# A four-layer decoder: bfloat16 parts of queries and keys, their way through DRAM, and the order of score banks

## The chip, the cores and the metric

The kernel runs on one core of one Trainium2 chip. The time is device microseconds (us) of that core, from one launch to its end. TensorE multiplies (PE in the profile), VectorE (DVE) and ScalarE (ACT) read its results from the PSUM banks, GpSimd (POOL) works on SBUF alone, and SyncE (SP) does nothing but issue DMAs, in a fixed order.

## What is computed

Four decoder layers on x of shape (4, 256, 128), each with self attention, a second attention on a context of 512 rows (or of x on it), and a feed-forward part, with residual sums and a layer norm without weights ahead of each. The change touches the attentions with 16 heads of width 8, above all those of layers 0 and 3:

```python
x = x + _L0_attn_ref(_layernorm(x, axis=-1), ...)
x = x + _L0_xattn_ref(_layernorm(x, axis=-1), ctx_1024, mask_BxS2_bk0, ...)
x = x + _L0_ffn_ref(_layernorm(x, axis=-1), ...)
...
x = x + _L3_attn_ref(_layernorm(x, axis=-1), L3_attn_mask, ...)
x = x + _L3_xattn_ref(_layernorm(x, axis=-1), ctx_1024, ctx_1024, mask_1x1xSxS2_if1, ...)
x = x + _L3_ffn_ref(_layernorm(x, axis=-1), ...)
```

and each attention is of this form:

```python
attn = jnp.einsum('bhqd,bhkd->bhqk', q, k) * scale
attn = jnp.where(mask, attn, -inf)
attn = jax.nn.softmax(attn, axis=-1)
out = jnp.einsum('bhqk,bhkd->bhqd', attn, v)
```

Self attention has 256 keys, attention on the context 512. Layer 1's self attention clips its scores at ±10 and so needs no maximum.

## The kernel before

`woven` (line 428) runs the attentions of one layer. A *unit* is one attention of one of the four batch elements: in layers 0 and 3 units 0 to 3 are self attention and 4 to 7 attention on the context; in layer 1 there are only the four self units.

**Two passes over the scores.** `rows_of` makes scores with queries on the partitions, and VectorE takes each row's maximum from them (L568, or L572 with a mask added). `parts` (L606 to L610) cuts the maximum into three bfloat16 pieces in `mp`, and `parts_T` transposes these on TensorE (L618 or L631). `columns_of` makes the same scores again with keys on the partitions, less the maximum, and ScalarE takes the exponential (L675). `weighted` (L708) multiplies it with the values, `divided_by_sums`, `transposed_result` and `added` end the unit.

**Slots and beats.** Slot n is the time of unit n's columns. Beside them run the rows of unit n+1, all but the first two half groups, and the first two half groups (`LEAD`) of unit n+2. A *beat* is one half group of rows with one half group of columns: two banks of each, on four different quarters of 32 rows of TensorE's array, which work side by side. A slot has 8 beats where both units have 256 keys, 16 with 512. `front(n)` puts the `prelude` of unit n+2 (its norm on POOL, transposes, query and key products) into the first 0.4 of the slot (0.55 with 512 keys), so that its rows can begin in the slot's last two beats.

**Parts.** A float32 matmul is slow on TensorE. In layers 0 and 3 (`split=True`) all units but the first take their scores from bfloat16 matmuls instead. ScalarE writes queries and keys in float32; POOL cuts each into three bfloat16 parts (`in_parts`, L470 to L473). A feature of a head needs three partitions for the key parts (i = 0, 1, 2) and a fourth for the maximum; the query has three planes c, each repeated on the three partitions. So the parts have to move between partitions, and go through DRAM: one DMA writes the query parts (L494), nine read them (L497, one for each plane and i), one writes the key parts (L515), three read them (L517); the row mask of the context goes into the fourth partition (L521). What the fourth partitions hold otherwise comes from the constant `rest`, by four loads for each of three buffers at the start (L461). A score is then three matmuls, one for each query plane (`part`, L579 for rows and L681 for columns). For columns the third plane is `qmax`: `parts_T` adds the maximum's pieces to a copy of it (L624).

A unit without parts masks the queries to one head on POOL (`qm`, L503), has one float32 matmul for a score (L561 for rows, L658 for columns), and for columns two more with bfloat16 pieces of the maximum (`less`, L652).

**What sets the order.** Each function of a slot has a place between 0 and 1, and `run` calls them sorted by it; a layer under the program places instructions on their engines' queues and makes the waits. SP issues in its own fixed order. The four loads of layer 0's expert weights into `e0h` (L2283, 1 MB each) are one of these functions, in slot 0. The buffers of the parts lie in memory lent by tiles that aren't in use yet (`Lent`): `e0h` in layer 0, `cn` and `w2kv` in layer 3, the rest in the pool as `kk` and `q`. So a tile named `e0h` in an attention's line is a buffer of parts.

**Banks.** `ps("s1")` takes the next of seven PSUM banks in rotation; a bank is free again when its reader is done. In `beat` (L763) the steps are called one after the other, and each takes its two banks; the matmuls then go in rounds over the steps, and the reads in pairs: first bank of the rows, first of the columns, second of the rows, second of the columns.

Of the kernel before, what the change touches and what calls it, by code (L numbers as in the profile page):

```python
# [26 lines left out]
F32 = mybir.dt.float32  # L27
# [9 lines left out]
P = 128  # L37
# [64 lines left out]
def _layout(i):  # L102
# [19 lines left out]
    halves = np.concatenate([np.where(d < 3, 0xBF80, 0), 0 * d, np.where(d == 3, 0x3F80, 0)])  # L122
    a["rest"] = np.tile((halves * 0x10001).astype(np.uint32).view(np.int32), (1, 2 * SK))
# [76 lines left out]
def decoder(ctx: ExitStack, tc: tile.TileContext, dr, out):  # L200
# [227 lines left out]
    def woven(pool, units, n_keys, split=False, lent=None):  # L428
# [4 lines left out]
        for i in range(2):  # L433
            t = pool.tile([P, n_keys // P, H, 32], F32, tag=f"v{i}", name=f"v{i}", bufs=1)
            V.memset(t, 0.0)
            V.memset(t[:, :, :, HD : HD + 1], 1.0)
            vbuf.append(t)
            shape = [P, 2, 4, 4, 32] if split else [P, 2, 4, 32]
            t = pool.tile(shape, BF16, tag=f"mp{i}", name=f"mp{i}", bufs=1)
            V.memset(t, 0.0)  # L440
            mbuf.append(t)
        if split:
            mfirst = pool.tile([P, 2, 4, 32], BF16, tag="mp", name="mp", bufs=1)
            V.memset(mfirst, 0.0)

        kbuf, qbuf, kd, qd = [], [], [], []
        for i in range(3 if split else 0):
            def kept(what, n):
                t = lent.pop(4 * n)
                if t is None:  # L450
                    return pool.tile([P, 4, n], BF16, tag=f"{what}{i}", name=f"{what}{i}", bufs=1)
                return t.rearrange("p (g n) -> p g n", g=4)

            kbuf.append(kept("kk", n_keys))
            qbuf.append([kept(f"q{c}", S) for c in range(3)])
            kd.append(dram.tile([3, P, n_keys], BF16, tag=f"kp{i}", name="kp"))
            qd.append(dram.tile([3, P, S], BF16, tag=f"qp{i}", name="qp"))
            for c, t in enumerate(kbuf[-1:] + qbuf[-1]):
                n = 4 * t.shape[2] // 2
                m = 32 * (0, 1, 1, 2)[c]  # L460
                nc.sync.dma_start(  # L461
                    t.bitcast(I32).rearrange("p g n -> p (g n)")[3::4],
                    dr["rest"][m : m + 32, :n],
# [15 lines left out]
        def queries(u):  # L479
# [11 lines left out]
            if u.split:  # L491
                u.q3 = qbuf[u.n % 3]
                to = qd[u.n % 3]
                nc.sync.dma_start(to.rearrange("c f n -> f c n"), in_parts(q, "qp", S))  # L494
                for c in range(3):
                    for i in range(3):
                        nc.sync.dma_start(  # L497
                            u.q3[c][i::4], to[c].rearrange("(x g) n -> x g n", g=4)
                        )
                return  # L500
            u.qm = pool.tile([P, 4, S], F32, tag="qm", name="qm", bufs=1 if split else 3)
# [3 lines left out]
        def keys(u):  # L505
            acc = product(u.weights[1], u.key_source, "s1")
            u.kc = pool.tile([P, u.nk], F32, tag="kc", name="kc", bufs=2 if split else 3)
            if u.k_bias is None:
                A.copy(u.kc, acc)
            else:  # L510
                A.activation(u.kc, acc, AF.Identity, bias=u.k_bias)
            if u.split:
                u.kk = kbuf[u.n % 3]
                to = kd[u.n % 3][:, :, : u.nk]
                nc.sync.dma_start(to.rearrange("c f n -> f c n"), in_parts(u.kc, "kp", SK))  # L515
                for c in range(3):
                    nc.sync.dma_start(  # L517
                        u.kk[c::4, :, : u.nk], to[c].rearrange("(x g) n -> x g n", g=4)
                    )
                if u.row_mask is not None:  # L520
                    nc.sync.dma_start(  # L521
                        u.kk[15::32, :, : u.nk],
                        u.row_mask[0:4].unsqueeze(1).to_broadcast([4, 4, u.nk]),
                    )

# [18 lines left out]
        def rows_of(u, qt, g, half):  # L544
# [5 lines left out]
            rounds, reads = {}, []  # L550
            for j, r in row_tiles(half):
# [1828 lines left out]
```

## Time and profile before

| | |
|---|---|
| three runs | 1535.40, 1537.69, 1541.26 us |
| median | 1537.69 us |
| the profiled execution | 1537.51 us, its span 1535.40 us |
| mean granted TensorE clock | 0.901 of full |
| TensorE busy (matmuls) | 1283.8 us, 84% |
| VectorE, ScalarE, GpSimd busy | 826.5, 721.7, 325.8 us |
| moved by DMA | 89.85 MB, 59 GB/s on average |

The span has these stages, by the names of the tiles in the timeline: layer 0's attentions from about 10 to 280 us, its experts to 360, layer 1 with its experts to 630, layer 2 to 1190, and layer 3 from there to the end. In forty slices of 38.4 us, busy tenths of TensorE, VectorE and ScalarE, and the granted clock:

```profile
PE   3677889797886999889999999999597488898894
DVE  6367877385565345755444544442333555776743
ACT  0243555566552334257766756666121034345463
PEclk9688999897887999999999999999698579999996
```

A 9 is 90% or more of a slice. The first seven slices are layer 0's attentions, the last nine layer 3. TensorE's clock is granted in two steps, full and half, so a tenth below 9 in the fourth line means that part of the slice ran at half clock.

### The profile page before, as it was taken

The numbers are of one execution on the slowest core, as the hardware profiler recorded it, in microseconds if no ns is written. First come the engines' busy times: TensorE is split into PE (matmuls) and PEld (weight loads), VectorE is DVE, ScalarE is ACT, GpSimd is POOL, SyncE is SP. The second block draws the span as 40 slices with busy tenths as digits, with TensorE's granted clock in tenths as the row PEclk, the third lists the DMA queues.
The fourth block names the chain that finished last, engine by engine and source line by source line (L and its number), as shares of the span: only waits on it lengthen the run. The fifth ranks groups of instructions, "written<-read, shape, count | busy, mean of one in ns | idle before, by whom it ended". The sixth has DMA issues, their size and how long they took to land.

```text
span 1535.4 us, 29900 instructions
## 1 busy us (share of the span) xinstructions
PE 1283.8 (84%) x11340; PEld 708.6 (46%) x11340; DVE 826.5 (54%) x2697; ACT 721.7 (47%) x1461; POOL 325.8 (21%) x489
## 2 busy tenths in 40 slices
PE   3677889797886999889999999999597488898894
PEld 2244444344344565645555555455365234344442
DVE  6367877385565345755444544442333555776743
ACT  0243555566552334257766756666121034345463
POOL 6133220155022315100000000000231613322000
PEclk9688999897887999999999999999698579999996
DMA  4232110331051216050110000000312211211000
GB/s 149 75 116 73 53 47 5 148 122 36 1 216 38 75 35 214 28 179 15 56 42 19 28 5 4 1 8 5 126 39 67 66 32 42 72 44 43 5 5 7
DMA packets 57263, 89.85 MB, mean 59 GB/s; under 512 B 8853, under 2 KB 35711, under 8 KB 55455
## 3 DMA queue, kind: packets, MB, share of 16 engines
q1 hardware_dynamic: 52706, 71.59, 14.1%
q0 software_dynamic: 3264, 6.69, 2.0%
q10 hardware_dynamic: 1152, 9.67, 1.6%
q8 instruction: 91, 1.49, 0.4%
q14 instruction: 50, 0.41, 0.1%
HBM read 64.10 MB, written 23.75 MB: 57 GB/s over the span
## 4 chain that ended last, share of the span: by engine, by line
PE 62%; DVE 12%; POOL 7%; ACT 6%; issue 5%; DMA 5%; SPq 2%; ACTq 0%; POOLq 0%; DVEq 0%
PE o L708 6%; PE o L2041 6%; PE g L1300 6%; PE s L579 5%; PE s L2021 5%; PE f L1967 4%; PE s L681 3%; PE y L1324 3%; PE s L645 2%; PE f L1953 2%; POOL xn L318 2%; PE s L360 2%; DVE mx L568 2%; POOL back L1373 2%; PE t L1309 2%
## 5 line engine op out<-in xcount | busy, mean ns | idle before, releaser
L675 ACT ACTIVATE pr<-s 128x512 f32<-128x512 f32 x384 | 206.4, 597 | 272.5 <-PE s L681 196.7
L310 POOL TENSOR_SCALAR ve<-mv 128x2 f32<-128x2 f32 x44 | 11.7, 267 | 776.7 <-DVE mv L305 771.2
L568 DVE TENSOR_REDUCE mx<-s 128x1 f32<-128x512 f32 (+1 forms) x192 | 122.2, 684 | 78.3 <-PE s L681 38.8
L1978 ACT ACTIVATE ss<-ss,ntop 128x768 f32<-128x768 f32 x128 | 118.6, 928 | 88.5 <-DVE ntop L1976 88.2
L708 PE MATMUL o<-pr,v 128*32 128x256 f32 (+1 forms) x1792 | 149.1, 404 | 7.4 <-ACT os L714 6.2
L1972 DVE CUSTOM_DVE_ANT_0 ss<-f,n 128x512 f32<-128x512 f32 x128 | 83.6, 689 | 73.7 <-PE f L1967 73.7
L579 PE MATMUL s<-e0h 32*128 32x512 bf16 (+1 forms) x672 | 80.6, 370 | 41.7 <-DMA e0h<-kp 37.1
L2041 PE MATMUL o<-pr,v 128*64 128x256 f32 x768 | 107.1, 392 | 1.2 <-ACT pr L2028 1.2
L572 DVE CUSTOM_DVE_ANT_0 junk<-s,nmif 128x512 bf16<-128x512 f32 x128 | 82.9, 687 | 37.8 <-PE s L681 30.1
L2021 PE MATMUL s<-qT,kT 64*128 64x256 f32 x768 | 101.5, 379 | 0.0
L2028 ACT ACTIVATE pr<-s,n 128x512 f32<-128x512 f32 x128 | 80.3, 679 | 24.5 <-PE s L2021 24.3
L1967 PE MATMUL f<-kT,qT 64*128 64x512 f32 x256 | 79.7, 637 | 3.7 <-ACT kT L290 2.0
L1278 POOL DMA_INDIRECT xb<-sent,token x62 | 59.8, 964 | 105.4 <-PE t L1285 58.8
L2041 PEld LDWEIGHTS o<-pr,v 128*64 128x64 f32 x768 | 48.0, 136 | 56.6 <-issue 20.3
L708 PEld LDWEIGHTS o<-pr,v 128*32 128x32 f32 x1792 | 41.4, 111 | 67.2 <-issue 45.5
L1960 DVE CUSTOM_DVE_ANT_0 ss<-f,nought 128x256 f32<-128x256 f32 x128 | 46.7, 421 | 46.7 <-PE f L1953 46.2
L2021 PEld LDWEIGHTS s<-qT,kT 64*128 64x128 f32 x768 | 67.8, 189 | 5.8
L572 DVE CUSTOM_DVE_ANT_0 junk<-s,nmcau 128x256 bf16<-128x256 f32 x128 | 46.4, 421 | 37.8 <-PE s L658 16.9
L579 PEld LDWEIGHTS <-e0h 32*128 32x128 bf16 x672 | 28.0, 100 | 76.0 <-issue 72.5
L681 PE MATMUL s<-e0h 32*128 32x256 bf16 x704 | 58.6, 283 | 4.8 <-DVE mx L568 4.6
L328 PE MATMUL s<-consts,xn 128*128 128x128 f32 x64 | 19.5, 361 | 47.2 <-POOL xn L318 47.2
L318 POOL TENSOR_SCALAR xn<-x,mv,rs 128x128 f32<-128x128 f32 x72 | 57.6, 807 | 3.8
(489 smaller groups left out, 2730.4 us busy)
## 6 DMA issues: line engine op xcount, KB each, us to landing
kd<-ahead SPq DMA_DIRECT2D x20, 256.0 KB
vd<-ahead SPq DMA_DIRECT2D x20, 256.0 KB
kT<-kd SPq DMA_DIRECT2D x20, 256.0 KB
v<-vd SPq DMA_DIRECT2D x5, 1024.0 KB
e0h<-in_e0h SPq DMA_DIRECT2D x4, 1024.0 KB
e0h<-in_e0h SPq DMA_DIRECT2D x1, 4096.0 KB
e0d<-in_e0d SPq DMA_DIRECT2D x2, 2048.0 KB
e1h<-in_e1h ACTq DMA_DIRECT2D x1, 4096.0 KB
```

The source lines that it names most:

```text
L318: (on or V).tensor_scalar(d, s, mv[:, i, 0:1], rs[:, i : i + 1], ALU.subtract, ALU.mult)
L568: V.tensor_reduce(u.mx[:, qt, j, g : g + per], sc, AX.X, ALU.max)
L572: V.tensor_tensor_reduce(junk[:, : u.nk], sc[:, i, :], u.rows_mask(qt), 1.0, -3e38, ALU.add, ALU.max, accum_out=u.mx[:, qt, j, g + i : g + ...
L579: T.matmul(sc[:, i, :], lhsT=u.q3[c][r, g + i, qt * P : (qt + 1) * P], rhs=u.kk[r, g + i, : u.nk], start=n == 0, stop=n == 3 * per - 1,)
L675: A.activation(dst, sc, AF.Exp)
L681: T.matmul(sc[:, i, :], lhsT=u.kk[r, gp + i, kt * P : (kt + 1) * P], rhs=(u.q3[0], u.q3[1], u.qmax)[c][r, gp + i, :], start=u.cols_mask is ...
L708: T.matmul(u.po[gp][32 * j : 32 * j + 32, i, first:], lhsT=u.v[:, kt, 4 * j + gp + i, :], rhs=u.pr[gp, kt, j][:, i, first:], start=kt + i ...
L1300: T.matmul(p[r], lhsT=xbT[b][:, r], rhs=w(512 * i), start=biases is None, stop=True,)
L1967: T.matmul(sc[h], lhsT=qT[u, c][hrow[h], qt * P : (qt + 1) * P], rhs=kT[u, c][hrow[h], :SK], start=True, stop=True,)
L1978: A.activation(ss[qt][h], ss[qt][h], AF.Exp, bias=ntop[:, qt, h, c : c + 1], accum_out=total[:, qt, h, c : c + 1],)
L2021: T.matmul(sc[h][:, i, :], lhsT=kT[u, c][hrow[h], kt * P : (kt + 1) * P], rhs=qT[u, c][hrow[h], :], start=False, stop=i == 1,)
L2041: T.matmul(po[u, g][hrow[h], i, :], lhsT=v[u][:, kt, n * hd : (n + 1) * hd], rhs=pr[u, g, kt, h][:, i, :], start=kt + i == 0, stop=kt + i ...
```

## The change

- Only units from 2 on are split into parts; unit 1 of layers 0 and 3 is computed as unit 0 is.
- In DRAM the parts now lie as they will lie in SBUF: partition 4x + i, and in it for the queries head group, plane and query in a row. Queries take three writes (one for each i, the same data) and one read, keys three writes (one for each part) and one read. The fourth partitions' constants are written into DRAM once for all three buffers, and the row mask goes there too, ahead of the read.
- The maximum's pieces are added to the third plane in place; `qmax` is gone. `mp3` is one tile for all split units. The float32 keys of split units have one buffer (`kf`).
- In a slot, the norm of unit n+3 comes at 0.8, and the rest of a split unit's prelude ends at 0.35 (0.5 with 512 keys) instead of 0.4 (0.55).
- `rows_of` and `columns_of` return a function for each bank instead of all banks; `beat` calls them in turn, one of either step, so banks are taken in the order in which they are read, and the matmuls of a round alternate between rows and columns.

```diff
+    words = [(h * 0x10001).astype(np.uint32).view(np.int32) for h in (
+        np.where(d < 3, 0xBF80, 0), np.where(d == 3, 0x3F80, 0)
+    )]
+    a["restk"] = np.tile(words[0], (1, 2 * SK))
+    n = np.arange(4 * 3 * S // 2)[None, :] // (S // 2) % 3
+    a["restq"] = np.where(n == 2, words[1], 0).astype(np.int32)
...
-    def woven(pool, units, n_keys, split=False, lent=None):
+    def woven(pool, units, n_keys, split=None, lent=None):
...
-            for c, t in enumerate(kbuf[-1:] + qbuf[-1]):
-                n = 4 * t.shape[2] // 2
-                m = 32 * (0, 1, 1, 2)[c]
+        if split:
+            kd = dram.tile([3, 32, 4, 4 * n_keys], BF16, tag=f"kp{split}", name="kp")
+            qd = dram.tile([3, 32, 4, 12 * S], BF16, tag=f"qp{split}", name="qp")
+            for i in range(3):
+                kbuf.append(kept(f"kk{i}", 4 * n_keys).rearrange("p (g n) -> p g n", g=4))
+                qbuf.append(kept(f"qq{i}", 12 * S).rearrange("p (g c n) -> p g c n", g=4, c=3))
+            for t, r in ((kd, dr["restk"]), (qd, dr["restq"])):
                 nc.sync.dma_start(
-                    t.bitcast(I32).rearrange("p g n -> p (g n)")[3::4],
-                    dr["rest"][m : m + 32, :n],
+                    t.bitcast(I32)[:, :, 3], r.unsqueeze(0).to_broadcast([3, 32, r.shape[1]])
                 )
...
             if u.split:
                 u.q3 = qbuf[u.n % 3]
-                to = qd[u.n % 3]
-                nc.sync.dma_start(to.rearrange("c f n -> f c n"), in_parts(q, "qp", S))
-                for c in range(3):
-                    for i in range(3):
-                        nc.sync.dma_start(
-                            u.q3[c][i::4], to[c].rearrange("(x g) n -> x g n", g=4)
-                        )
+                to, t = qd[u.n % 3], in_parts(q, "qp", S).rearrange("p c n -> p (c n)")
+                for i in range(3):
+                    nc.sync.dma_start(to[:, i].rearrange("x (g n) -> x g n", g=4), t)
+                nc.sync.dma_start(
+                    u.q3.rearrange("p g c n -> p (g c n)"), to.rearrange("x i n -> (x i) n")
+                )
                 return
-            u.qm = pool.tile([P, 4, S], F32, tag="qm", name="qm", bufs=1 if split else 3)
+            u.qm = pool.tile([P, 4, S], F32, tag="qm", name="qm", bufs=2 if split else 3)
...
             if u.split:
                 u.kk = kbuf[u.n % 3]
-                to = kd[u.n % 3][:, :, : u.nk]
-                nc.sync.dma_start(to.rearrange("c f n -> f c n"), in_parts(u.kc, "kp", SK))
-                for c in range(3):
-                    nc.sync.dma_start(
-                        u.kk[c::4, :, : u.nk], to[c].rearrange("(x g) n -> x g n", g=4)
-                    )
+                to = kd[u.n % 3].rearrange("x i (g n) -> x i g n", g=4)[:, :, :, : u.nk]
+                t = in_parts(kc, "kp", SK)
+                for i in range(3):
+                    nc.sync.dma_start(to[:, i], t[:, i])
                 if u.row_mask is not None:
                     nc.sync.dma_start(
-                        u.kk[15::32, :, : u.nk],
+                        to[3::8, 3],
                         u.row_mask[0:4].unsqueeze(1).to_broadcast([4, 4, u.nk]),
                     )
+                nc.sync.dma_start(u.kk[:, :, : u.nk], to.rearrange("x i g n -> (x i) g n"))
...
-                u.qmax = pool.tile([P, 4, S], BF16, tag="qmax", name="qmax")
-                V.tensor_tensor(
-                    u.qmax, tp.rearrange("p (g n) -> p g n", g=4), u.q3[2], ALU.add
-                )
+                third = u.q3[:, :, 2, :]
+                V.tensor_tensor(third, tp.rearrange("p (g n) -> p g n", g=4), third, ALU.add)
                 return
...
-            made = [f(half) for f, half in steps]
+            pairs = zip(*[f(half) for f, half in steps])
+            made = [f() for pair in pairs for f in pair]
...
-            for pair in zip(*[m[2] for m in made]):
-                for f in pair:
-                    f()
+            for _, _, read in made:
+                read()
...
-                end = 0.95 - lead if not u.split else 0.4 if units[n].nk < SK else 0.55
-                out += spread(prelude(u), 0.0, end)
+                if u.split:
+                    end = 0.35 if units[n].nk < SK else 0.5
+                    out += spread(prelude(u)[1 if n else 0 :], 0.0, end)
+                else:
+                    out += spread(prelude(u), 0.0, 0.95 - lead)
+            if split and n + 3 < len(units):
+                out += [(0.8, prelude(units[n + 3])[0])]
...
-            u.n, u.split = n, split and n > 0
+            u.n, u.split = n, bool(split) and n > 1
...
-            first += spread(prelude(units[1]), 0.0, 0.3 if split else 0.8)
+            first += spread(prelude(units[1]), 0.0, 0.8)
```

## The prediction

> **What bounds the kernel now.** I read the page for the span and the engine shares, then the waits, then PE's timeline over the two stages that call `woven` with parts (layer 0, about 10 to 280 us, and layer 3, about 1190 us to the end), then SP's timeline for one unit, then windows around one stop.
>
> ```profile
> PE 1283.8 (84%) x11340; PEld 708.6 (46%) x11340; DVE 826.5 (54%) x2697; ACT 721.7 (47%) x1461; POOL 325.8 (21%) x489
> L579 PE MATMUL s<-e0h 32*128 32x512 bf16 (+1 forms) x672 | 80.6, 370 | 41.7 <-DMA e0h<-kp 37.1
> ```
>
> TensorE is the engine that carries the span, and the score rows (L579) are the one group that stands idle on a DMA. The tile view of kp gives PE's whole wait on it as 55.4 us in 10 stops. PE's timeline shows the stops:
>
> ```profile
> 45.16 1.25 PE L579 MATMUL s<-e0h 32*128 32x256 bf16 x19 [13.17 <-DMA e0h<-kp]
> 72.76 0.39 PE L579 MATMUL s<-e0h 32*128 32x256 bf16 x2 [5.88 <-DMA e0h<-kp]
> 101.25 0.39 PE L579 MATMUL s<-e0h 32*128 32x256 bf16 x2 [7.32 <-DMA e0h<-kp]
> 128.35 0.61 PE L579 MATMUL s<-e0h 32*128 32x512 bf16 x2 [6.84 <-DMA e0h<-kp]
> 192.04 0.61 PE L579 MATMUL s<-e0h 32*128 32x512 bf16 x2 [3.50 <-DMA e0h<-kp]
> 229.35 0.61 PE L579 MATMUL s<-e0h 32*128 32x512 bf16 x2 [4.62 <-DMA sent<-xn]
> 1256.19 0.40 PE L579 MATMUL s<-kk,q 32*128 32x256 bf16 x2 [5.42 <-DMA kk<-kp]
> 1286.14 0.39 PE L579 MATMUL s<-cn 32*128 32x256 bf16 x2 [7.00 <-DMA cn<-kp]
> 1315.03 0.61 PE L579 MATMUL s<-w2kv 32*128 32x512 bf16 x2 [5.38 <-DMA w2kv<-kp]
> ```
>
> Each is the first row matmul of a new unit; in brackets is how long PE stood before it. Their sum is 59.1 us, 41.3 in layer 0 and 17.8 in layer 3. (The one put down to `sent` has SP's three kp reads issued just ahead of it; I count it as theirs.) Why the parts are late is on SP:
>
> ```profile
> 114.20 0.36 SPq L494 DMA_DIRECT2D qp<-qp  x1
> 116.17 5.59 SPq L497 DMA_DIRECT2D e0h<-qp  x9
> 121.86 0.53 SPq L515 DMA_DIRECT2D kp<-kp  x1
> 124.50 1.72 SPq L517 DMA_DIRECT2D e0h<-kp  x3
> ```
>
> Query write, 1.97 us until its nine reads may issue, 5.59 us to issue them, then the key write behind them, though POOL had the key parts at 117.9; 2.64 us to land, three reads, and PE starts at 128.35: 14.15 us. A stop costs twice, as the granted clock (last but two column) shows around the one at 66.9 to 72.8:
>
> ```profile
> 70.00:72.00 2.00, 0.00 (x0) 0.00 (x0) 0.00 (x0) 0.00 (x0) 0.00 (x0) 0.92 0.27 79
> 72.00:74.00 2.00, 1.24 (x18) 0.94 (x20) 0.00 (x0) 0.00 (x0) 0.00 (x0) 0.50 0.37 72
> 76.00:78.00 2.00, 2.00 (x17) 0.84 (x19) 1.68 (x5) 0.27 (x1) 0.00 (x0) 0.50 1.04 430
> 78.00:80.00 2.00, 2.00 (x31) 0.90 (x24) 0.41 (x1) 0.56 (x2) 0.00 (x0) 0.87 0.98 414
> ```
>
> **What the skill says.** The Trainium skill, "TensorE: Matmul & The Clock Gate", "What's actually happening": after an idle window of about 3.4 us the array gets half its clock, and full clock again after a busy one. The trace agrees: 0.50 from the stop until about 78.5. "DMA: Bandwidth & Descriptors", "Anatomy of one DMA — SWDGE (gpsimd) path": a DMA costs about 2.0 us plus its bytes at 436 GB/s, most of the fixed part being the wait for the write's receipt. The page fits another issuing path, but here 192 KB of queries takes 1.97 us and the 384 KB key write 2.64, and the windows move 414 to 430 GB/s; I use 2.0 and 430. The page's "Rules for kernel authors" say to coalesce many small transfers into one large; the one read does that.
>
> **The change part by part.**
>
> *Units split.* Unit 1 of either layer stays in float32. The 13.17 us stop goes, but its rows still wait for VectorE: in the trace the last row reduction of unit 0 ends at 35.0; four banks of unit 1 at 0.64 us (L568) and the copy of mT follow, so slot 0 can start at about 38.7 instead of 49.4: 10.7 gained. In layer 3 unit 1 had no DMA stop. Price: the columns of unit 1. A beat's score matmuls take 0.84 us when both sides are parts (81.77 to 82.61) and 1.34 with float32 columns (62.50 to 63.84): 0.5 x 8 beats x 2 layers = 8. Mixed float32 rows and columns in slot 0 I put at 0.15 x 6 x 2 = 1.8 more, an estimate: the second row matmul stands ahead of the column's second correction in PE's order. Six transposes less per layer give back 1.6. On POOL, four masks of queries (3.63) replace eight part operations (4.2 to 4.3): nothing. In layer 3 they stand behind the norm of unit 2 and its gathers in POOL's order: I allow 2 us. Sum +10.
>
> *Writes and reads.* Per split unit the queries take three writes and one read in place of one and nine; the keys three and one in place of one and three. From POOL's finished queries (at 430 GB/s, issues 0.36 to 0.53 us as in the trace): three writes issue in 1.1 and land at 2.7; the read issues until 3.3 and moves 786 KB, landing at about 7.1. Key parts are ready at 3.7, each write waits for its own part, the last issues by 4.6 and lands at about 7; the read of 524 KB issues by 7.6 and lands at 7.6 + 1.2 + about 1.7 = 10.5. That is 3.6 less than 14.15. Bounds: 9 if nothing queues on the rings, 16 if the wider reads move at the 105 GB/s of the nine small ones (576 KB in 5.59 us). I take 10.5, since the 430 GB/s windows show large rows at full rate.
>
> *Begun sooner.* The norm moves to 0.8 of the slot before, and in PE's order both products come one beat sooner: about 2.0 us. With 3.6 this covers 5.6 us of each stop. But full clock at a slot's head also shortens the slot before the parts are needed. Counting beats from the key product to the first row of the unit: unit 3 of layer 0 has 4 x 1.25 + 3.6 of weighted sums + 2 = 10.6 us against a chain of 9 to 10; unit 4 has 8.0 against 0.7 + 3.6 + 2.6 + 0.5 + 3.2 = 10.6. Unit 2's reads now stand behind the first 1 MB load of `e0h` (2.4 us). Left over: unit 2 about 2, unit 3 about 1, unit 4 about 2.6; in layer 3 about 0, 0.5 and 2; the later cross units none (3.50 and 4.62 are under 5.6). So 8 us stay, and of 59.1 go 59.1 - 2.5 (VectorE, unit 1) - 8 = 48.6. The other three `e0h` loads (3 MB, 7.5 us) now precede unit 3's writes on their semaphores, but more than a slot's half lies between: nothing; if the cover went, up to 7 us.
>
> *Clock.* Behind the stops before, PE worked at half clock for 5.8, 4.65, 4.85, 6.0, 6.25 (layer 0) and 3.4, 4.3, 6.0 us (layer 3): 41.3. Half would be lost if PE alone set the pace; I take 0.4: 16.5. Slot 0 of layer 0 stood at half clock until about 61.6: five beats at 3.4 us (52.23 to 55.63) that take 2.56 warm (62.50 to 65.06): 4.3. Less 3 for the stops left over: 17.8. The head of layer 3 keeps its low clock (0.51 over 1180 to 1240), where VectorE waits for gathers.
>
> *Bank order, and the rest.* Banks are now allocated as they are read, so a reused bank frees in order. PE's waits on readers at L579 and L681 are about 25 us in all, few of them of this kind: -3 to +1, taken as 0. The third plane is added in place; were the first plane's matmuls to wait for it too, 0.5 us x 12 units: 0 to +6, taken as 0, since the list has under 3 us for the wait on `qmax`. `kf` has one buffer instead of two, but its next writer comes a slot later: nothing. One more `evacuate` swaps VectorE and ScalarE for the copies between the two layers; both have slack there (PE's digit is 9 in most of those slices of the page): -2 to +2.
>
> Sum: 48.6 + 17.8 - 10 = 56. The profiled execution took 1537.51 us with a span of 1535.40, 2.1 around it, and the median shown is 1537.69: 1537.5 - 56 = 1481.5, so **1482 us**. A check: layer 0 from 40 to 240 us has VectorE busy for 132.2 us. It loses about 44 of its 200 us; 132/156 is 85%, and the undisturbed stretch 140 to 180 already has 34.7 of 40 (87%). So this is near the next bound, and much more is not to be had there.
>
> **The rivals.**
>
> *Half of it stays.* PE reaches the row beats sooner than counted, so most split units still stop 2 to 4 us, long enough to halve the clock. For it: unit 4's count; against: 5.6 us per unit. Nine stops of 3 us and their clock: 27 + 9 left instead of 8 + 3, so gain 56 - 25 = 31: 1507.
>
> *All of it goes.* No stop is left, and the clock stays: 56 + 11 = 67, and bank order gives 3 to 8: about 1465. VectorE's 87% speaks against it.
>
> *Slower.* The threefold writes and the wide reads move at the small reads' 105 GB/s. Per unit 590 + 786 + 393 + 524 KB = 2.3 MB: 22 us and two receipts of 2: 26 against 14.15. Twelve units, less the 2 us begun sooner, late by 10 more each, 120, less the 25 that unit 1 gives: about 1620. It decides once the chain passes about 17 us: 2.9 more than 14.15, less 2.0, in 12 units is 11, as much as unit 1's gain after its price. Below some 180 GB/s it wins; the windows with 414 to 430 speak against.
>
> **How the numbers follow.** Forecast 0.62 (1465 to 1500), half of it 0.19, all of it 0.09, slower 0.06, no change 0.04 (the gains met by VectorE). The range 1458 to 1512 holds the first three but for their edges. This kernel's runs tell 0.5%, some 8 us, from no change: faster 0.90, same 0.04, slower 0.06.
>
> **What would show it.** PE's line at L579 with DMA waits under 15 us in all instead of 55; SP's chain from the first query write to the key read's landing near 10.5; no cold stretch in slot 0 of layer 0; beats of unit 1's columns near 1.3 us. It is wrong if stops of over 3 us stay before unit 3 or 4, if the single reads take over 6 us to land, or if VectorE is over 90% busy in layer 0.

## The result

The changed kernel takes 1518.4 us (median of four runs, 1512.65 to 1520.42) beside 1537.0 (1535.40 to 1541.26): ratio 0.9869, 95% interval 0.9835 to 0.9902, so 18.6 us faster where 56 were forecast. The profiled execution took 1517.87, its span 1516.0, with a mean granted clock of 0.912. From the page after (engine shares; then the group of row matmuls, with its idle time and releaser last):

```profile
PE 1292.0 (85%) x11200; PEld 709.5 (47%) x11200; DVE 821.6 (54%) x2696; ACT 722.7 (48%) x1462; POOL 324.1 (21%) x481
...
L582 PE MATMUL s<-e0h 32*128 32x512 bf16 (+1 forms) x576 | 73.0, 365 | 18.8 <-DMA e0h<-kp 18.3
```

and PE's timeline after, each line the first row matmul of a unit:

```profile
61.11 0.37 PE L582 MATMUL s<-e0h 32*128 32x256 bf16 x1 [5.08 <-DMA e0h<-kp]
92.57 0.37 PE L582 MATMUL s<-e0h 32*128 32x256 bf16 x1 [5.26 <-DMA e0h<-kp]
117.67 0.58 PE L582 MATMUL s<-e0h 32*128 32x512 bf16 x1 [5.48 <-DMA e0h<-kp]
179.97 0.48 PE L582 MATMUL s<-e0h 32*128 32x512 bf16 x1 [2.46 <-DMA e0h<-kp]
1241.58 0.33 PE L582 MATMUL s<-kk,qq 32*128 32x256 bf16 x1 [2.47 <-DMA kk<-kp]
1268.58 0.26 PE L582 MATMUL s<-cn,w2kv 32*128 32x256 bf16 x1 [2.25 <-DMA cn<-kp]
1293.72 0.58 PE L582 MATMUL s<-cn,qq 32*128 32x512 bf16 x1 [2.78 <-DMA cn<-kp]
```

These are units 2, 3, 4 and 6 of layer 0 and 2, 3, 4 of layer 3: 25.8 us of stops beside 59.1 before. The forecast left 8.

A stop is a difference of two times, both counted from the first query write on SP: the *chain*, until the parts have landed, less the *cover*, until PE has nothing else to do. Read off SP's and PE's timelines (us; layer 3's units with a dash ahead):

```
             unit:    2      3      4      6      7     -2     -3     -4
before      chain  14.03  14.66  14.15  14.67  15.29  13.89  14.22  14.71
            cover   8.15   7.34   7.31  11.17  10.67   8.47   7.22   9.33
after       chain  13.07  17.07  11.17  14.71     no   8.87  12.78  11.04
            cover   7.99  11.81   5.69  12.25   stop   6.40  10.53   8.26
```

Forecast were a chain of 10.5 and 2.0 more cover everywhere. Over the seven units that still stop the chain went from 14.3 to 12.7 and the cover from 8.4 to 9.0: 2.2 us off each stop, not 5.6. (Unit 7, whose stop went, is not in these means.) And the longest chain is longer than any before. SP's timeline after, for unit 3 of layer 0:

```profile
75.50 1.85 SPq L496 DMA_DIRECT2D qp<-qp  x3
77.44 2.07 SPq L520 DMA_DIRECT2D kp<-kp  x3
79.56 0.74 SPq L463 DMA_DIRECT2D qp<-in_restq  x1
80.47 0.35 SPq L497 DMA_DIRECT2D e0h<-qp  x1
80.93 0.56 SPq L526 DMA_DIRECT2D e0h<-kp  x1
```

The third line is layer 3's constant. It depends on nothing, so it was placed 1100 us ahead of its use, and right before unit 3's reads. Windows of the same kernel (stretch, length, PE, PEld, DVE, ACT, POOL busy, then the granted clock, the share of the 16 DMA engines that is busy, GB/s):

```profile
86.00:88.00 2.00, 1.07 (x16) 0.42 (x16) 1.86 (x6) 0.19 (x1) 2.00 (x4) 1.00 0.18 74
88.00:90.00 2.00, 0.00 (x0) 0.00 (x0) 0.14 (x1) 0.00 (x0) 1.65 (x3) 1.00 0.20 83
90.00:92.00 2.00, 0.00 (x0) 0.00 (x0) 0.00 (x0) 0.00 (x0) 0.00 (x0) 0.84 0.19 70
```

0.18 to 0.20 of 16 engines is three. The constant has the three buffers as its outermost dimension, and the Trainium skill, "DMA: Bandwidth & Descriptors", "Rules for kernel authors", says that an outermost dimension of c < 16 keeps a whole DMA on at most c engines. The trace agrees. It also shows what follows: unit 3's key read was issued at 80.93, from 86 us on only about three engines still work, at some 75 GB/s, and PE starts at 92.57. A read that is spread over all engines is then complete only when those three have worked off the 576 KB that stand ahead of it in their queues, the *rings*; consts_later, below, tests this.

### The profile page after: what moved, and what is told of

It is laid out like the page before. It is cut to its first block, busy times and chain, and to the rows that moved or that the text cites. A ratio compares the mean times of both kernels' runs of the same rounds, so it can differ in the third digit from the quotient of the medians.

```text
span 1516.0 us, 29457 instructions
## 1 busy us (share of the span) xinstructions
PE 1292.0 (85%) x11200; PEld 709.5 (47%) x11200; DVE 821.6 (54%) x2696; ACT 722.7 (48%) x1462; POOL 324.1 (21%) x481
## 3 DMA queue, kind: packets, MB, share of 16 engines
q1 hardware_dynamic: 46318, 77.61, 14.8%
## 4 chain that ended last, share of the span: by engine, by line
PE 62%; DVE 10%; ACT 8%; DMA 7%; POOL 7%; issue 5%; SPq 1%; ACTq 0%; POOLq 0%; DVEq 0%
PE o L2040 6%; PE g L1299 6%; PE o L701 5%; PE s L2020 5%; PE f L1966 4%; PE s L582 4%; PE y L1323 3%; PE s L679 3%; PE f L1952 2%; PE s L643 2%; DMA e0h<-kp 2%; DVE mx L571 2%; PE s L656 2%; PE t L1308 2%; PE s L2013 2%
## 5 line engine op out<-in xcount | busy, mean ns | idle before, releaser
L314 POOL TENSOR_SCALAR ve<-mv 128x2 f32<-128x2 f32 x44 | 10.7, 243 | 743.6 <-DVE mv L309 738.6
L582 PE MATMUL s<-e0h 32*128 32x512 bf16 (+1 forms) x576 | 73.0, 365 | 18.8 <-DMA e0h<-kp 18.3
L679 PE MATMUL s<-e0h 32*128 32x256 bf16 x960 | 68.4, 273 | 3.6 <-DVE mx L571 2.2
L656 PE MATMUL s<-qm,kc 32*128 32x512 f32 (+1 forms) x256 | 64.3, 710 | 0.0
L575 DVE CUSTOM_DVE_ANT_0 junk<-s,nmcau 128x256 bf16<-128x256 f32 x128 | 46.2, 421 | 32.9 <-PE s L656 15.0
```

The source lines that it names most:

```text
L575: V.tensor_tensor_reduce(junk[:, : u.nk], sc[:, i, :], u.rows_mask(qt), 1.0, -3e38, ALU.add, ALU.max, accum_out=u.mx[:, qt, j, g + i : g + ...
L582: T.matmul(sc[:, i, :], lhsT=u.q3[r, g + i, c, qt * P : (qt + 1) * P], rhs=u.kk[r, g + i, : u.nk], start=n == 0, stop=n == 3 * per - 1,)
L656: T.matmul(sc, lhsT=u.kc[r, kt * P : (kt + 1) * P], rhs=u.qm[r, gp : gp + 2, first:], start=u.clip, stop=True,)
L679: T.matmul(sc[:, i, :], lhsT=u.kk[r, gp + i, kt * P : (kt + 1) * P], rhs=u.q3[r, gp + i, c, :], start=u.cols_mask is None and n == 0, stop ...
```

## The experiments

The kernel before ran beside every group: 1537.1, 1533.1, 1548.1, 1534.6 and 1537.2 us in groups 1 to 5. The one tried kernel that ran twice, wide_kf_sooner and again as best_again, took 1484.2 and 1483.1. Whether medians or ratios carry better from one group to another isn't known, so I give both, and where a few us matter I go by kernels of one group or by the trace. "Stops" is the sum of the stops of over 1 us on parts; in the three kernels of the change that have unit 1 split (wide_unit1split, best_unit1split, layout_only) 14.8 to 16.4 of it stand before unit 1, before the change 13.2.

```
                  group  median   ratio   95% interval     stops
before                   1537.0                             59.1
after                    1518.4  0.9869  0.9835 0.9902      25.8
before_unit1        1    1535.9  0.9999  0.9975 1.0022      45.9
old_banks           1    1514.3  0.9854  0.9802 0.9907      28.4
consts_wide         1    1508.1  0.9815  0.9774 0.9857      22.4
loads_late          1    1516.9  0.9874  0.9824 0.9924      28.1
consts_later        2    1508.3  0.9843  0.9810 0.9876      22.6
wide_unit1split     2    1510.4  0.9849  0.9821 0.9878      38.8
wide_oldtime        2    1524.0  0.9938  0.9915 0.9962      37.0
wide_kf_sooner      2    1484.2  0.9673  0.9637 0.9710       9.2
wide_keysfirst      3    1506.7  0.9735  0.9695 0.9774      13.1
wide_sooner         3    1491.6  0.9628  0.9594 0.9661      11.2
best_oldbanks       3    1485.4  0.9584  0.9553 0.9616       4.5
best_earlier        3    1487.6  0.9627  0.9585 0.9670       4.1
best_again          4    1483.1  0.9661  0.9635 0.9687       6.7
best_unit1split     4    1490.7  0.9721  0.9688 0.9754      27.1
layout_only         4    1523.0  0.9917  0.9886 0.9948      53.7
best_loads6         4    1484.8  0.9664  0.9637 0.9692       5.7
after_turn          5    1507.9  0.9804  0.9779 0.9830      28.0
best_turn           5    1481.2  0.9628  0.9604 0.9653       8.3
```

**What stands in the rings.** Three kernels move it:

```diff
 loads_late
-            units[0].beside += [loads]
+            units[6].beside = [loads] + units[6].beside
 consts_wide
-                    t.bitcast(I32)[:, :, 3], r.unsqueeze(0).to_broadcast([3, 32, r.shape[1]])
+                    t.bitcast(I32)[:, :, 3].rearrange("x f n -> f x n"),
+                    r.unsqueeze(1).to_broadcast([32, 3, r.shape[1]]),
 consts_later (c is the constant's DMA)
+                if split == "l3":
+                    tc.keep_in_program_order(c)
```

> The changed kernel with the four 1 MB loads of layer 0's expert weights moved from slot 0 to slot 6, where no parts travel. Theory 1 (unit 2's reads land late since 1 MB goes ahead of them and 3 MB beside them): the stop before unit 2 falls from 5.08 us to about 2.5, the half-clock stretch of 17 us at slot 1 to 7 or less, and the time by 5 to 8 us to about 1512. Rival (the chain of writes and reads alone is as long as that): the stop stays over 4 us, the time at 1516 to 1521.

> The changed kernel with the two constants for the fourth partitions written with the 32 features as the outermost dimension instead of the 3 buffers; same bytes, same places in the order. Theory 1 (the write with 3 outermost runs on 3 of the 16 DMA engines: 74 to 83 GB/s at a busy share of 0.18 to 0.20 while layer 3's 576 KB precede unit 3's reads; 32 outermost spreads it): the stop before unit 3 falls from 5.26 us to under 1, its half-clock stretch goes, and the time falls by 6 to 9 us to about 1511. Rival (unit 3 waits for its own chain of writes and reads): the stop stays over 4 us and the time at 1516 to 1521.

> The changed kernel with one thing changed: layer 3's two constants (384 and 576 KB, still with the 3 buffers as the outermost dimension) are held in their place in the program, at the start of layer 3, and no longer go out in slots 0 and 1 of layer 0. The expert loads stay in slot 0. Theory 1 (these constants in the rings are what holds unit 3's reads): unit 3's stop falls from 5.26 us to 4 or less, its chain from 17.1 to about 12.5, slot 1 from 31.5 us to 24 to 27, and the time to 1508 to 1513. Rival (consts_wide gained by its queue order, which also put the expert loads at the very start): unit 3's chain stays over 16 us and the time at 1516 to 1521.

The loads are not it. They have no dependency either and still went out in slot 0, but all behind unit 2's reads: that chain fell from 13.07 to 11.86, PE came 0.9 us earlier too, and the stop was 4.80. Half clock there fell to 6.8 us, as theory 1 has it, and the time stayed. The constants are. PE's timeline of consts_later:

```profile
84.50 0.26 PE L584 MATMUL s<-e0h 32*128 32x256 bf16 x1 [3.63 <-DMA e0h<-kp]
```

Unit 3's chain is 12.39, though its query read now goes ahead of the key writes (75.73 and 76.18 us on SP). Slot 1 lasts 23.5 us instead of 31.5, and the trace is 9.8 us ahead of the changed kernel's at slot 7. consts_wide, which also had the loads at the very start, gives the same chain and slot (12.47, 23.7); its stop of 3.72 was to fall under 1 and didn't. Both medians are 10 us under the changed kernel's; by ratio it is 4 us for consts_later and 8 for consts_wide, with intervals that overlap the changed kernel's, so the slot shows the cause better than the times do. Not all of slot 1's 8 us is the constants': the changed kernel also had 17.1 us of half clock from 57.2 on, where these two have 6.8. after_turn, below, has the constants in place and 6.8 us of half clock there, and its slot 1 takes 29.0: so some 5.5 us are the constants' and 2.5 the clock's. With 32 outermost the constants run at full width; windows of best_loads6, where layer 0's constants have the rings to themselves:

```profile
16.00:18.00 2.00, 0.00 (x0) 0.00 (x0) 2.00 (x17) 0.00 (x0) 2.00 (x5) 1.00 0.87 257
18.00:20.00 2.00, 0.00 (x0) 0.00 (x0) 0.56 (x5) 0.00 (x0) 2.00 (x5) 0.82 0.71 290
```

The changed kernel moves 57 to 83 GB/s there, from 16 to 30 us.

best_loads6 is wide_kf_sooner with the loads as in loads_late and held there with `keep_in_program_order`:

> wide_kf_sooner with the four expert loads held in slot 6 (in that kernel the scheduler had put them at the very start). Theory 1 (nothing of them was left in the rings by unit 2's reads): same within 2.5 us, unit 2's stop 3 to 4 us. Rival (a ring free of them shortens the start): 3 to 6 us faster.

As theory 1 has it: loads in slot 6 change nothing once the rest is in order.

**Unit 1 alone.** Kernel before, and consts_wide and wide_kf_sooner the other way round:

```diff
-            u.n, u.split = n, split and n > 0
+            u.n, u.split = n, split and n > 1
-            first += spread(prelude(units[1]), 0.0, 0.3 if split else 0.8)
+            first += spread(prelude(units[1]), 0.0, 0.8)
```

> The kernel before with one part of the change: unit 1 of layers 0 and 3 unsplit (float32), its products due by 0.8; small buffers are arranged to make room (float32 keys of split units in one buffer, one mp for split units, one buffer of key parts). All other units as before. Theory 1 (the prediction's own terms: 10.7 won at the start of layer 0, 4.3 by slot 0 at full clock, 10 paid for float32 columns): 1537.0 - 5 = about 1532. Rival (the price is larger, since slot 1 with its float32 columns is met at half clock): the start still wins about 11 us, but slots 0 and 1 together lose 12 or more in layer 0 and 3 to 5 more are lost in layer 3: 1537 to 1545.

> consts_wide (1508.1 us) with unit 1 of layers 0 and 3 split into parts again, its prelude due by 0.3 as before. Theory 1 (the prediction's price: 10.7 us at the start and 4.3 of half clock in slot 0 won, 10 paid): 5 us slower, about 1513. Second theory (the trace of before_unit1: 13 us won in layer 0, 2 to 4 lost in layer 3): 9 to 12 us slower, 1517 to 1520, with the first 13 us stop back. Rival (unit 1 is worth nothing, as the median of before_unit1 has it): 1505 to 1510.

> wide_kf_sooner with unit 1 of both layers split again. Theory 1 (the prediction's price: start and slot 0 won 15, float32 columns paid 10): 5 us slower than best_again. Rival (the price is near 15, so unit 1 gains nothing): within 2.5 us, with slots 0 and 1 of layer 0 shorter by 4 us or more together and slots 0 and 1 of layer 3 by 2 to 4.

In the median before_unit1 wins nothing. Its trace is 11.8 us ahead where slot 0 begins (34.74 beside 46.56) and 13.3 at slot 7, but the warmer slot 0 gives unit 2 less cover:

```profile
60.88 0.39 PE L581 MATMUL s<-e0h 32*128 32x256 bf16 x2 [8.43 <-DMA e0h<-kp]
```

(5.88 before), and the trace is only 7.5 ahead at layer 3's slot 0. Where the stops are small, splitting unit 1 again costs 7.7 us (best_unit1split beside best_again, one group); beside the large stops 2.3 (medians of two groups; 5 by ratio). The forecast's net of 5 lies between. Its price for the columns, 4 us in each layer, can be read in slot 1, which holds them: in layer 0 it takes 21.8 us with float32 columns and 19.9 without, but 2.75 of the 19.9 are a stop before unit 3, so about 4.7; in layer 3, without such a stop, 23.3 and 21.9, so 1.4.

**Chain, times and queue order.** layout_only keeps only the new way through DRAM; wide_oldtime is consts_wide with the old times; the others go on from consts_wide:

```diff
 layout_only: unit 1 split, the old times, the old bank order
 wide_oldtime
+                    end = 0.4 if units[n].nk < SK else 0.55
+                    out += spread(prelude(u), 0.0, end)
 wide_sooner, wide_kf_sooner (best_earlier: 0.1 and 0.25)
+                    end = 0.2 if units[n].nk < SK else 0.4
+                    out += spread(prelude(u)[1:], 0.0, end)
...
+            first += [(0.9, prelude(units[2])[0])]
 wide_keysfirst, wide_kf_sooner (in keys(u), behind the three key writes)
+                tc.keep_in_program_order(nc.sync.dma_start(
+                    u.q3.rearrange("p g c n -> p (g c n)"), u.read.rearrange("x i n -> (x i) n")
+                ))
```

> Only the new way through DRAM (writes, one read each, in-place third plane; constants 32 outermost): unit 1 split, old times of the prelude, old bank order. Theory 1 (the prediction's chain: 14.15 to 10.5 us, 3.6 less in each of nine stops, and part of their clock): 35 to 42 us faster than the kernel before, ratio 0.973 to 0.977. Rival (without the timing and with the query read ahead of the key writes the chain only falls to 12.5 or 13): 12 to 20 us faster, 0.987 to 0.992, stops of 3 us and more left before nearly every unit.

> consts_wide (1508.1 us) with the old times of the prelude: all of it in the slot before (ends at 0.4 and 0.55) and no norm at 0.8 of the slot ahead. Theory 1 (the prediction: both products come one beat, 2.0 us, sooner for every unit): seven stops 2.0 us longer and their clock, 14 + 4 us slower: about 1526. Rival (only where the place of the query product crosses a beat, unit 3 and the units beside 512 keys, does anything come sooner; unit 4's query writes already come 11.65 us into the slot as against 11.55 before): stops of units 2 and 4 as long as in consts_wide within 0.5 us, those of units 3, 6 and 7 longer by 2: 5 to 9 us slower, 1513 to 1517.

> consts_wide with one thing changed: the query read of every split unit is issued behind the unit's three key writes (the mask write ahead of them). Theory 1 (a 768 KB read ahead of the key writes on SP and in the rings costs units 3, 6 of layer 0 and 3 of layer 3 about 2 to 3 us of chain): their stops fall from 3.7, 2.4 and 2.3 us to under 1.7, 0.5 and 0.5, those of units 2 and 4 (5.7 and 5.6) stay; 6 to 9 us faster than consts_wide, ratio to the kernel before about 0.976. Rival (the query read that comes later lands later, nothing is won): within 3 us of consts_wide, 0.980 to 0.983, and the gain of wide_kf_sooner is the timing alone.

> consts_wide with one thing changed: the preludes end at 0.2 and 0.4 of the slot and unit 2's norm comes before slot 0; the order of reads and writes is left to the scheduler. Theory 1 (cover: query products one beat sooner where they weren't): covers of units 2, 4 and of layer 3 grow by 2 to 2.5 us and their stops shrink by as much; 14 to 18 us faster than consts_wide, ratio about 0.971. Rival (cover without a shorter chain is worth half of wide_kf_sooner's gain): about 0.975, with a chain over 12 us left where a query read precedes its key writes.

> consts_wide (1508.1 us) with the query read always issued behind the three key writes, and the prelude sooner: ends at 0.2 and 0.4 of the slot, and unit 2's norm before slot 0. Theory 1 (the stops are chain less cover: the query read of 768 KB ahead of the key writes costs units 3, 6, 7 about 3 us of chain, and query products that cross one beat more give 2 us of cover or more): stops of units 6 and of layer 3 go, those of units 2, 3, 4 (5.7, 3.7, 5.6 us) fall to 3 or less, no chain over 13 us; 15 to 20 us faster, 1488 to 1493. Rival (VectorE or the norm on GpSimd then ends last): the DMA stops go, others take their place, 1500 to 1508.

> wide_kf_sooner with the preludes ending at 0.1 and 0.25 of the slot, the four expert loads held until slot 6 and layer 3's constants until layer 3 (both in their place in the program). Theory 1 (cover and a free ring are all that is missing): the last three stops (4.0, 3.2, 2.0 us) go, chain of unit 2 under 10 us, 8 to 13 us faster than wide_kf_sooner, ratio 0.959 to 0.962. Rival (the norm on GpSimd and VectorE's reductions are then what TensorE waits for at the heads of slots): 0.965 to 0.972, with new waits of 1 to 3 us on xn, xnT or mx in the heads of slots.

layout_only is 11.6 us faster than its group's kernel before, ratio 0.9917: the rival, at its lower edge. PE's timeline of it:

```profile
97.05 0.40 PE L583 MATMUL s<-e0h 32*128 32x256 bf16 x2 [7.61 <-DMA e0h<-kp]
122.35 0.61 PE L583 MATMUL s<-e0h 32*128 32x512 bf16 x2 [7.34 <-DMA e0h<-kp]
```

Chains over the same eight units are 12.7 us on average (14.45 before), and the cover is 7.8 (8.7 before), since slots with less half clock end sooner. Why 12.7 and not 10.5 is in SP's order, here unit 6 in the changed kernel:

```profile
165.26 1.81 SPq L496 DMA_DIRECT2D qp<-qp  x3
170.55 0.33 SPq L497 DMA_DIRECT2D e0h<-qp  x1
170.92 1.84 SPq L520 DMA_DIRECT2D kp<-kp  x3
176.78 0.33 SPq L526 DMA_DIRECT2D e0h<-kp  x1
```

SP waits for the query writes to land before it issues the read, and the key writes, whose parts POOL had at 169.9, stand behind: on SP, and then in the rings behind 768 KB. That is the very pattern of before, with one read in place of nine. In wide_kf_sooner:

```profile
149.59 2.20 SPq L497 DMA_DIRECT2D qp<-qp  x3
151.84 1.98 SPq L524 DMA_DIRECT2D kp<-kp  x3
154.04 0.40 SPq L525 DMA_DIRECT2D e0h<-qp  x1
155.47 0.33 SPq L529 DMA_DIRECT2D e0h<-kp  x1
```

The key read issues 5.9 us after the first write instead of 11.5. wide_keysfirst has this alone: the stops before unit 3, 6 and layer 3's unit 3 go, those of 2 and 4 stay (4.95, 5.25), as theory 1 says. Its ratio agrees (0.9735 beside 0.9815), but by the medians of two groups it wins only 1.4 us, so its worth in time stays uncertain. Within group 3 the order, added to the sooner times, makes 6 us (wide_sooner 1491.6, best_oldbanks 1485.4, which has the old bank order besides), and the times, added to the order, 21 (from wide_keysfirst's 1506.7 to the same 1485.4).

The times are worth much: wide_oldtime is 16 us slower than consts_wide in medians and has 14.6 us more of stops, near theory 1. But not as "one beat for every unit": for the six units that stop in both, the cover is 2.1 us less in consts_wide for unit 2, and 1.6, 0.4 and 1.0 more for units 3, 4 and 6 of layer 0, 2.3 and 0.6 more for units 3 and 4 of layer 3. A prelude of four or five functions is spread over the slot's first part, and each runs ahead of the beat whose place comes next. For unit 4 of layer 0 (five functions) the query product has place 0.28 before and 0.22 after; the beats stand at 0.19 and 0.31, so it runs ahead of the same beat: its first write comes 11.55 us into the slot before, 11.68 after, and its cover is 5.69. Only the key product moved. wide_sooner puts the query product over the next beat: the stops before units 2 and 4 fall to 2.75 and 3.68, and one chain of 14.5 (unit 6, the read ahead again) is left. Both edits together leave

```profile
55.31 0.37 PE L586 MATMUL s<-e0h 32*128 32x256 bf16 x1 [4.04 <-DMA e0h<-kp]
100.78 0.58 PE L586 MATMUL s<-e0h 32*128 32x512 bf16 x1 [3.17 <-DMA e0h<-kp]
1262.16 0.37 PE L586 MATMUL s<-cn,qq 32*128 32x512 bf16 x1 [1.97 <-DMA cn<-kp]
```

9.2 us, at chains of 10.8 to 12.0, and 1484.2 us: 24 less than consts_wide, more than theory 1 asked. Still sooner (best_earlier, with loads and constants held late as well) wins nothing: 3 us less in layer 0, but slots 0 and 1 of layer 3 take 23.1 and 24.3 us instead of the 20.4 and 23.3 of best_again. No DMA stop and no wait of 1 us stands in these two slots; half clock reaches 12.2 us into slot 0 instead of 5.7. Why it does is open.

**Bank order.**

```diff
-            pairs = zip(*[f(half) for f, half in steps])
-            made = [f() for pair in pairs for f in pair]
+            banks = [[f() for f in step(half)] for step, half in steps]
+            made = [m for bank in banks for m in bank]
```

> The changed kernel with the banks taken again as before: both banks of a step together, reads in pairs. Theory 1 (bank order moves nothing, as the prediction has it): 1515 to 1521, slots of split units within 0.5 us. Rival (the new order is what lost 3 us in layer 3's later slots, which have no DMA stop, and some in every slot): 4 to 10 us faster, 1508 to 1514, with slot 3 of layer 3 (units 3 and 4, no DMA stop in it) at 30.4 us as before instead of 31.7.

> wide_kf_sooner (ratio 0.9673) with the banks taken as before the change: both banks of a step together, reads in pairs. Theory 1 (bank order moves nothing): 0.965 to 0.970, slots 4 to 6 of either layer within 0.5 us. Rival (the new order costs, as the median of old_banks, 4 us under the changed kernel, would have it): 0.961 to 0.964. Other rival (the new order gains once the stops are gone): over 0.970.

> wide_kf_sooner once more, beside the next three on one chip, since the kernel before took 1533 to 1548 us in different calls. Both theories: 1481 to 1488. Against best_oldbanks (1485.4): if the bank order is worth nothing, within 3 us of it; the rivals there have it 4 us or more to either side.

old_banks is 4 us under the changed kernel, between its two theories and with intervals that overlap, and its layer 3 slots 3 to 5 (29.6, 36.2, 47.4 us) differ from the changed kernel's (31.7, 36.2, 46.2) both ways. best_again and best_oldbanks are 2.3 us apart in medians; their slots 4 to 6 of layer 0 are 30.59, 31.12, 32.17 and 30.58, 31.11, 32.17 us. Nothing that shows, then, where nothing else differs; their ratios can't be set beside each other, as the kernel before differs by 0.9% between the groups.

**The turn of the copies.** `evacuate` gives copies to VectorE and ScalarE in turn. Unit 1 in float32 has one more (mT), which swaps all that follow. Ahead of the kernel before by 18.6 us at slot 7 of layer 0, the changed kernel is 14.7 ahead at the first transpose of layer 3.

```diff
             evacuate(u.mT, tp[:, :S])
+            if split and u.n == 1:
+                turn[0] ^= 1
```

> The changed kernel with one thing changed: after unit 1's one more copy (the transposed maximum) the turn between VectorE and ScalarE is set back, so that every later copy in layers 1 to 3 falls to the engine that had it before the change. Theory 1 (the swapped copies cost the 4 us that the changed kernel loses against the kernel before between layer 0's end and layer 3's head, above all near 870 us of the span): the advance over the kernel before at the head of layer 3 is as large as at the end of layer 0, within 1 us, and the time is 3 to 5 us less, about 1514. Rival (the loss is chance or comes from half clock): a loss of 2 us or more stays in layers 1 and 2, time 1516 to 1521.

> wide_kf_sooner with the same single edit. Theory 1 (the swapped copies cost 3 us in layer 2, as best_again lost 37.7 - 34.6 = 3.1 us there while best_unit1split and layout_only, with unit 1 split and so one copy less, lost under 1 near 870 us): no step near 870 us of the span, 2 to 4 us faster than wide_kf_sooner, 1479 to 1482. Rival: 1483 to 1487 with the step still there.

after_turn is 10.5 us faster than the changed kernel, more than theory 1 asked, with intervals that don't meet. It is 18.6 us ahead at slot 7 and 18.5 at layer 3, and the wait in the changed kernel's PE timeline

```profile
862.28 1.62 PE L1966 MATMUL f<-kT,qT 64*128 64x512 f32 x2 [1.14 <-ACT kT L294]
```

behind which 6.8 us of half clock began, is gone. In layer 3 another 7 us come back, 4.5 of them in slot 0 (23.1 us instead of 27.6). But half clock reaches 4.2 us into that slot instead of 11.8, and best_again and best_earlier, both with the swap, differ in the same way (5.7 and 12.2 us of half clock, 20.4 and 23.1 us). So how much of the 10.5 is the copies' isn't shown. The traces give a smaller figure over layer 2 (657 to 1085 us in the kernel before), if the same matmuls are matched: thirteen of the fourteen kernels with the swap lose 1.4 to 3.1 us of their lead there (best_loads6 7.0), after_turn 0.6, best_turn 1.4, the three that split unit 1 at most 0.4. With wide_kf_sooner the edit gives 2 to 3 us in medians, with intervals that overlap, and without the step near 870: **best_turn, 1481.2 us, ratio 0.9628 (0.9604 to 0.9653)**, the lowest median of all.

## Why the prediction was wrong

**Right.** Unit 1 unsplit moved slot 0's start by 11.2 us (46.56 to 35.34), as against 10.7; the head of layer 3 lost 2.4 of its lead, as against 2. No DMA stop is left before unit 1. Bank order is worth nothing that shows. And the kernels with 8.3 and 9.2 us of stops took 1481.2 and 1484.2, where the sum had 8 us of stops for 1482. That is in part luck: best_oldbanks and best_earlier, with 4.5 and 4.1 us of stops, took 1485.4 and 1487.6, and terms of the sum were off both ways.

**Writes and reads: the step that failed.** The chain was to fall from 14.15 to 10.5 us; over the seven units it fell from 14.3 to 12.7, so 1.7 us came off instead of 3.6, and 33 us of the 59.1 of stops went where 51 were to.

"The read issues until 3.3 ..., the last [key write] issues by 4.6" has each issue go out about when its data are ready. In unit 6 the query writes took 5.3 us to let their read go, not 2.7; the key writes, ready by 4.6, stood behind that waiting read on SP and began at 5.7; the key read issued at 11.5, not 7.6. Sorted by what SP has ahead, the seven chains are 8.9, 11.0 and 11.2 where the key writes go before the query read and nothing else is in the way (units 2 and 4 of layer 3, unit 4 of layer 0; in the first, one key write goes out 1.6 us before the count begins), 12.8 and 14.7 where the query read goes first (unit 3 of layer 3, unit 6), 13.1 behind the first 1 MB load (unit 2, the one that the prediction named) and 17.1 with layer 3's constants ahead of the reads (unit 3).

So 10.5 is near the chain that nothing holds up; the step took it from the diff, and the order of SP's instructions holds most units up. The 414 to 430 GB/s that it leaned on are no rate of parts: SP had issued the four expert loads at 72.75, just ahead of these windows. Parts come near it, at 345 to 373 GB/s for unit 6 (173 to 175 and 178 to 179 us), so the rate isn't what failed. The constants were worth 5.5 us in slot 1, and 4 to 10 in all. Their outermost dimension is in the diff, and the page cited for another rule warns of it. The slow rate that the rival "Slower" spoke of did occur, in a DMA that it didn't name, and its point of decision, a chain of 17 us, was reached by one of the seven.

**Begun sooner: too large as well.** "Both products come one beat sooner" holds for unit 3 and beside 512 keys, not for the query product of units 2, 4 and 5 of layer 0. The cover grew by 0.6 us on average instead of 2.0, so that "this covers 5.6 us of each stop" measured 2.2. Query products that do cross a beat, together with the key writes ahead of the query read, are worth 24 us in medians (consts_wide to wide_kf_sooner).

**Clock.** 17.8 us were counted for it. In layer 0's attentions half clock went from 68 us to 44, and 11 of the 24 lay in unit 1's stop, where nothing ran. Slot 0 was forecast to have no cold stretch: it has 10.2 us of it from 36.7 on, without a DMA stop, behind a wait of 0.96 us for VectorE (mp) and at the start of one of 1.25 (mT). The Trainium skill, "TensorE: Matmul & The Clock Gate", "What's actually happening", fits a stop of 5 us that costs its clock; it doesn't fit this wait, nor the half clock of the last section.

**The rest.** "Evacuate ... -2 to +2" was 10.5 us in medians, of which the traces place 3.8 in layers 1 and 2. The constants' 10 and these 10.5 would leave 16 of the 36 us that were missing, if they add and if the medians may be taken whole; no run has just these two. The nearest rival was "Half of it stays", with 27 us of stops (25.8 measured); its 1507 is 11 under the measured time. L579 was not quite the one group that stands idle on a DMA: L1285 stood 6.6 us on gathers, outside these layers.

## What to carry to other kernels

For a transfer through DRAM, read the issue order of the queue in the built kernel and list all that stands ahead of each read, in the queue and in the rings, constants of later stages too: what depends on nothing is placed anywhere. Put the writes of all parts ahead of the first read that waits for a write. Where functions are spread over places between beats, an earlier end moves nothing until a place crosses a beat; count it for each unit.

## What the runs showed of the hardware

Half clock can outlast its stop by far. In the changed kernel, after the stop that ended at 61.1 us, windows show

```profile
64.00:66.00 2.00, 2.00 (x23) 1.26 (x21) 1.59 (x6) 0.61 (x2) 0.00 (x0) 0.50 1.02 426
70.00:72.00 2.00, 2.00 (x12) 0.70 (x10) 1.29 (x2) 1.08 (x2) 0.00 (x0) 0.50 0.19 80
```

and full clock only from 74.3: 13 us with PE busy for 96% or more of every 2 us from 62 on. In consts_later, after a stop of 6.2 us at the same place, it took 4 us. What makes the difference stayed open. The trace's records of the granted clock hold full and half and nothing between, and in the changed kernel every stretch of half clock is a whole multiple of 3.41 us (3.4, 6.8, 10.2, 17.1), whatever the stop before it.

A read that waits for its writes on SP holds up every write behind it, ready or not: with the key writes ahead of it, unit 6's key read issued at 5.9 us instead of 11.5. And three writes of 192 KB take SP 1.8 us to issue, 0.6 each, where the single one of before took 0.36.
